# Causal attention between two feed-forward blocks: which of two score tiles comes first, and when VectorE reads it

## The chip, the core and the metric

The kernel runs on one core of a Trainium2 chip. The core has a matrix engine (TensorE, "PE" in the profile, with its weight loads as "PEld"), a vector engine (VectorE, "DVE"), a scalar engine (ScalarE, "ACT"), GpSimd ("POOL") and a sync engine (SyncE, "SP") whose queue issues the DMA transfers here. Matrix products go to PSUM, which the kernel uses as eight banks of 128 partitions x 512 fp32. VectorE and ScalarE read them from there. The metric is the device time of one execution in microseconds, as the median of several runs. Everything is fp32, but for a small operand of zeros.

## The reference

The program computes `x + ffn/2`, then `x + attention`, then `x + ffn/2` again, over 16 sequences of 512 tokens and 256 channels. The change touches the attention alone:

```python
def _L0_attn_ref(x, Wq, bq, Wkv, bkv, Wo, bo):     # x: layernormed, 16 x 512 x 256
    q = x @ Wq + bq                                  # H = 16 heads, DQK = DV = 64
    k, v = jnp.split(x @ Wkv + bkv, [H * DQK], axis=-1)
    q = _rope(q.reshape(b, s, H, DQK).transpose(0, 2, 1, 3))
    k = _rope(k.reshape(b, s, H, DQK).transpose(0, 2, 1, 3))
    v = v.reshape(b, s, H, DV).transpose(0, 2, 1, 3)
    scores = jnp.einsum('bhqd,bhkd->bhqk', q, k) * (1.0 / np.sqrt(DQK))
    scores = jnp.where(causal[None, None], scores, -jnp.inf)
    probs = jax.nn.softmax(scores, axis=-1)
    out = jnp.einsum('bhqk,bhkd->bhqd', probs, v)
    return out.transpose(0, 2, 1, 3).reshape(b, s, H * DV) @ Wo + bo
```

## The kernel before

**Units.** The work is cut into 64 units: a sequence and a group of four of its 16 heads (`units`, `HG = 4`). A unit's 512 queries are four tiles of 128 (0 to 3). Since the mask is causal, tile i needs only the first (i + 1) x 128 keys, so its score rows are 128, 256, 384 and 512 wide.

**The loop.** One loop (`for u in range(-2, nu)`, `L1221`) runs over the units as a pipeline, and each turn works on several units at once. In this part of the program the order of the instructions on every engine is the order in which the source writes them: nothing is rescheduled. In a usual turn TensorE does, in this order:

- `sums(u, 0)` and `sums(u, 1)` (`L1162`): probabilities times values for unit u, `p_av`, one bank for two heads; ScalarE moves each bank to `oT` by three activations (`L1183`);
- the scores of tiles 3 and 2 of unit u + 2, each in four banks, one a head (`scores`, `by_halves`, `L1063` and `L1070`);
- `leave(u, 0)` and `leave(u, 2)` (`L1185`): the output product `p_ay`, a bank each, which VectorE adds to `x` later in the turn (`L1196`);
- queries and keys of unit u + 3, four banks (`L988`); the values of unit u + 1, two banks (`L1010`); the scores of tiles 1 and 0 of unit u + 2, four banks (`L1048`).

That makes 22 banks a turn. They are handed out in turn from a ring of eight (`ps`, `L56`), so each product takes the bank of the one made eight before it, and waits until that one has been read. In the turn before the change, `leave(u, 0)` takes the bank of head 0 of tile 3, `leave(u, 2)` that of head 1, and heads 2 and 3 of tile 2 take the banks of the two `sums`.

**A score tile by halves.** For tiles 2 and 3, `by_halves` makes a head's 128 queries as two sides of 64, on the two column halves of the array, and the four heads lie on four groups of 32 rows. The later queries need 64 more keys than the earlier ones, so the sides are 320 and 384 wide for tile 2, and 448 and 512 for tile 3. Where the short side lacks 64 columns, a matmul of zeros (`blank`, `L1063`) fills them first. All four blanks of a tile come ahead of its other matmuls. For tile 3 the sides are swapped (`turned`), so that the side with the blank is the upper half there and the lower half in tile 2. The loop `for half in (1, 0)` gives the order in which the two sides are issued.

**Softmax.** `exps` (`L1074`) goes by head: VectorE scales and masks the scores out of the bank and takes the row's extreme (`L1086`), ScalarE does the exponential and its row sum (`L1090`). `scaled` (`L1093`) takes the reciprocals on VectorE and multiplies the rows on GpSimd (`L1098`).

**Turning.** The probabilities must be transposed for `sums`. VectorE turns blocks of 32 x 32 into `sq` (`L1113`): `turn_most` for a head's tiles 2 and 3, `turn_corner`, `turn_tile(1)` and `turn_tile(0)`. Then `move` (`L1132`) issues 16 DMA transfers on SP that put the blocks in place in `prT` (`L1140`). There is one buffer of `sq` for the unit being moved, so `turn_most(0)` of the next unit, at the end of the turn, waits for these transfers.

**VectorE's order around the change** (`old` is unit u + 1, `new` is unit u + 2): turns of `old` up to `turn_corner` and `turn_tile(1)`; the read of head 0 of `new`'s tile 3; `turn_tile(0)` and `move`; the reads of heads 1, 2 and 3 of tile 3; the four reads of tile 2, with the reciprocals of tile 3 halfway; the two additions of `p_ay`; the reciprocals of tile 2; the token statistics; the rotations of q and k (`L994`); `turn_most(0)`; the reads of tiles 1 and 0.

Of the kernel before, what the change touches and what calls it, by code (L numbers as in the profile page):

```python
# [34 lines left out]
HG = 4  # L35
# [12 lines left out]
def macaron_kernel(ctx: ExitStack, tc: tile.TileContext, a: dict, out: bass.AP):  # L48
# [836 lines left out]
    def attention(qp, wq, wk, wv, wo, cos, sin, row):  # L885
# [25 lines left out]
        nu = len(units)  # L911
# [19 lines left out]
        def enter(b):  # L931

            hs[b] = [qp.tile([P, 2, D], F32, tag=f"rope{2 + k}", name=f"h{b}_{k}") for k in range(2)]
            for t in range(NT):
                i = (b % PB) * NT + t
                nc.scalar.activation(hs[b][t // 2][:, t % 2, :], xs[b][:, t, :], AF.Identity,
                                     bias=shifts[b // PB][:, i:i + 1], scale=rstds[b // PB][:, i:i + 1])
# [5 lines left out]
        def width(b):  # L943
            hTs[b] = qp.tile([P, NC, S], F32, tag="hT", name=f"ahT{b}", bufs=2)
            for c in range(NC):
                pt = ps(f"p_ahT{b}_{c}")
                for t in range(NT):
                    nc.tensor.transpose(pt[:, t * P:(t + 1) * P], hs[b][t // 2][:, t % 2, c * P:(c + 1) * P], ident)
                nc.scalar.copy(hTs[b][:, c, :], pt)  # L949
# [52 lines left out]
        def values(u, t0):  # L1002
            b, hg = units[u]
            if t0 == 0:
                pool, tag, bufs = (ap, "v", 1) if u + 1 < nu else (qp, "hT", 2)
                vs[u] = pool.tile([P, NT, HG * DQ], F32, tag=tag, name=f"v{b}_{hg}", bufs=bufs)
            pv = ps(f"p_v{b}_{hg}_{t0}")
            for t in range(2):
                for k in range(NC):
                    nc.tensor.matmul(pv[:, t * 256:(t + 1) * 256], hTs[b][:, k, (t0 + t) * P:(t0 + t + 1) * P],  # L1010
                                     wv[:, k, hg * HG * DQ:(hg + 1) * HG * DQ],
                                     start=(k == 0), stop=(k == NC - 1))
            nc.scalar.copy(vs[u][:, t0:t0 + 2, :].rearrange("p t d -> p (t d)"), pv)  # L1013
# [8 lines left out]
        class Weights:  # L1022
# [33 lines left out]
            def by_halves(self, i, q, k, banks, at):  # L1056


                w, turned = (i + 1) * P, int(i == NT - 1)
                early = slice(turned * H, (turned + 1) * H)  # L1060
                for j in range(HG):
                    zero = blank[j * 32:(j + 1) * 32, :]
                    nc.tensor.matmul(banks[j][early, at + w - H:at + w], zero, zero, start=True, stop=True)  # L1063
                for n in range(2):
                    for j in range(HG):
                        rows = slice(j * 32, (j + 1) * 32)
                        for half in (1, 0):
                            late = half ^ turned
                            q0, wh = i * P + late * H, w - (1 - late) * H
                            nc.tensor.matmul(banks[j][half * H:(half + 1) * H, at:at + wh],  # L1070
                                             q[n][rows, q0:q0 + H], k[n][rows, :wh],
                                             start=(n == 0), stop=(n == 1))
# [131 lines left out]
        def queries_keys(u):  # L1204

            if u >= nu:
                return []
            q = qs[u] = Rotated(u, "q", wq, R_BQ)
            k = ks[u] = Rotated(u, "k", wk, R_BK)
            return [lambda: q.half(0), lambda: (q.half(1), q.add()), lambda: k.half(0), lambda: (k.half(1), k.add())]  # L1210
# [7 lines left out]
        with tc.tile_pool(name="awayh", bufs=2, space=bass.MemoryType.DRAM) as away, \  # L1218
                tc.manual_schedule(engines={mybir.EngineType.DVE, mybir.EngineType.Activation,
                                            mybir.EngineType.Pool, mybir.EngineType.SP}):  # L1220
            for u in range(-2, nu):  # L1221
                new = ws[u + 2] = Weights(u + 2) if u + 2 < nu else None
                qk = queries_keys(u + 3)
                old = ws.get(u + 1)

                fresh = units[u + 5][0] if NHG < u + 5 < nu and units[u + 5][1] == 0 else 1 if u + 3 == NHG else None

                stats = [divmod(at, NHG) for at in range(seen, min(u + 15, NB * NHG))]
                seen = max(seen, u + 15)
                left = [divmod(u - NHG - 1, NHG)] if u >= NHG + 1 else []  # L1230
                if u + 2 == nu:
                    old.scaled((1, 0))
                    values(u + 1, 0)
                    values(u + 1, 2)
                if u >= 0:
                    sums(u, 0)
                    sums(u, 1)
                if fresh:
                    enter(fresh)
                if u + 4 in trips:  # L1240
                    trips[u + 4].land((0, 1))
                if u + 3 in trips:
                    trips[u + 3].land((2, 3))
                if old and u + 2 == nu:
                    old.turn_at_once("sq", range(0, 10, 2))
                elif u == -1:
                    values(0, 0)
                    values(0, 2)
                    old.turn_at_once("prT", range(2, 10, 3))
                elif old:  # L1250
                    old.scaled((1, 0), slice(0, HG // 2))
                    old.turn_most(1)
                    old.turn_most(2)
                    old.scaled((1, 0), slice(HG // 2, HG))
                    old.turn_most(3)
                    old.turn_corner()
                    old.turn_tile(1)
                if new:
                    new.scores((3,))
                    new.scores((2,))  # L1260
                    new.exps((3,), slice(0, 1))
                if old and 0 <= u < nu - 2:
                    old.turn_tile(0)
                    old.move()
                if new:
                    new.exps((3,), slice(1, 2))
                gone = [leave(u, 0)] if u >= 0 else []
                if fresh == 1:
                    width(1)
                if u >= 0:  # L1270
                    gone.append(leave(u, 2))
                if new:
                    new.exps((3,), slice(2, HG))
                    new.exps((2,), halfway=lambda: new.scaled((3,)))
                if u == -2:
                    new.scaled((2,))
                    new.scores((1, 0))
                    new.exps((1, 0))
                    new.scaled((1, 0))
                if u + 6 in stds:  # L1280
                    scales((u + 6) // (PB * NHG), stds.pop(u + 6))
                if fresh and fresh > 1:
                    trips[u + 5] = Trip(fresh)

                if u == nu - NHG + 1:
                    for g in range(NB // PB - 1):
                        pair_rstd(g)
                if u == nu - 1:
                    for g in range(PB):
                        entered[g] = xs[g]  # L1290
                        for t in range(NT):
                            i = (g % PB) * NT + t
                            nc.vector.tensor_scalar(xs[g][:, t, :], xs[g][:, t, :], mvs[g // PB][:, i, 0:1],
                                                    rstds[g // PB][:, i:i + 1], ALU.subtract, ALU.mult)
                for one in gone:
                    one()
                if new and u > -2:
                    new.scaled((2,))
                for one in stats + left:
                    token_stats(*one)  # L1300
                for one in qk:
                    one()
                if fresh:
                    with_bias(fresh)
                if NHG < u + 7 < nu and (u + 7) % (PB * NHG) == 0:
                    stds[u + 7] = spread((u + 7) // (PB * NHG))
                if 0 <= u < nu - 2:
                    values(u + 1, 0)
                    values(u + 1, 2)
                if new and u > -2:  # L1310
                    new.scores((1, 0))
                    if u + 3 < nu:
                        new.turn_most(0)
                    new.exps((1, 0))
            token_stats(NB - 2, NT - 1)
# [55 lines left out]
```

## Time and profile before

| what | us |
|---|---|
| median of three runs | 2301.3 (2299.74 to 2306.26) |
| the profiled execution | 2299.63 |
| its span, first to last instruction | 2297.9 |
| one turn of the loop (1005.90 to 1029.16) | 23.26 |
| of it, `sums` to the scores of tile 3 (1007.42 to 1011.88) | 4.46 |
| the scores of tiles 3 and 2, to `p_ay` (1011.88 to 1015.19) | 3.31 |

The page gives, for each engine, the time in which it was busy over the whole program and its share of the span. The tables of windows give the same for stretches of time. A timeline line has the start and length of a merged group of instructions, and in brackets how long the engine had been idle before it and who released it. Matmuls are pipelined, and their ends are modelled: a following group can start a little before the end shown for the one ahead.

### The profile page before, as it was taken

The numbers are of one execution on the slowest core, as the hardware profiler recorded it, in microseconds if no ns is written. First come the engines' busy times: TensorE is split into PE (matmuls) and PEld (weight loads), VectorE is DVE, ScalarE is ACT, GpSimd is POOL, SyncE is SP. The second block draws the span as 40 slices with busy tenths as digits, with TensorE's granted clock in tenths as the row PEclk, the third lists the DMA queues.
The fourth block names the chain that finished last, engine by engine and source line by source line (L and its number), as shares of the span: only waits on it lengthen the run. The fifth ranks groups of instructions, "written<-read, shape, count | busy, mean of one in ns | idle before, by whom it ended". The sixth has DMA issues, their size and how long they took to land. (4 is left out here: it accounts for less than half of the span.)

```text
span 2297.9 us, 47763 instructions
## 1 busy us (share of the span) xinstructions
PE 2243.8 (98%) x16984; PEld 1463.8 (64%) x16984; DVE 1764.6 (77%) x4678; ACT 1158.2 (50%) x3296; POOL 1068.5 (47%) x1695
## 2 busy tenths in 40 slices
PE   7999999999999999999999999999999999998999
PEld 4764488666666666666666666666666666764588
DVE  5742298788989898989898998989888875432387
ACT  5753243555555555556465655555555565632233
POOL 2210053565566556565656565656656552210053
PEclk9999999999999999999999999999999999999999
DMA  6839851044545454454544454536454443839734
GB/s 213 260 108 406 347 141 56 9 131 120 135 123 152 107 153 127 125 139 112 146 130 129 129 143 110 159 97 163 119 134 129 124 116 113 238 141 406 306 117 141
DMA packets 221909, 359.19 MB, mean 156 GB/s; under 512 B 99876, under 2 KB 159848, under 8 KB 213480
## 3 DMA queue, kind: packets, MB, share of 16 engines
q1 hardware_dynamic: 220812, 355.34, 52.4%
q8 instruction: 135, 2.21, 0.4%
q10 hardware_dynamic: 860, 0.81, 0.1%
q14 instruction: 102, 0.84, 0.1%
HBM read 156.29 MB, written 37.22 MB: 84 GB/s over the span
## 5 line engine op out<-in xcount | busy, mean ns | idle before, releaser
L1098 POOL TENSOR_SCALAR pr<-pr,ars 128x512 f32<-128x512 f32 (+3 forms) x1024 | 524.1, 532 | 566.3 <-DVE ars L1095 565.3
L1090 ACT ACTIVATE pr<-pr,amn 128x512 f32<-128x512 f32 (+3 forms) x1024 | 561.9, 550 | 211.5 <-DVE amn L1086 207.1
L1113 DVE STREAM_TRANSPOSE sq<-pr 128x768 f32<-128x768 f32 x434 | 384.5, 918 | 78.6 <-DMA prT<-sq 54.8
L1013 ACT COPY v<-p_v 128x512 f32<-128x512 f32 x128 | 74.6, 585 | 449.4 <-PE p_v L1010 449.4
L1171 PE MATMUL p_av<-prT,v 128*64 128x512 f32 (+3 forms) x2048 | 289.8, 436 | 1.4 <-ACT pr L1090 1.4
L1086 DVE CUSTOM_DVE_ANT_1 pr<-p_as,causal 128x384 f32<-128x384 f32 (+1 forms) x512 | 237.8, 483 | 44.0 <-PE p_as L1048 43.6
L1190 PE MATMUL p_ay<-wo,aoT 128*128 128x256 f32 x1024 | 238.5, 386 | 12.0 <-DVE amn L1086 12.0
L1086 DVE CUSTOM_DVE_ANT_0 pr<-p_as,causal 128x512 f32<-128x512 f32 (+1 forms) x512 | 235.2, 478 | 2.7 <-PE p_as L1070 2.7
L1190 PEld LDWEIGHTS p_ay<-wo,aoT 128*128 128x128 f32 x1024 | 189.4, 190 | 70.3 <-DVE amn L1086 46.9
L1010 PE MATMUL p_v<-wv,ahT 128*128 128x256 f32 x1024 | 231.6, 379 | 0.7 <-DVE x L1196 0.7
L988 PE MATMUL p_q<-ahT,wq 128*128 128x512 f32 x512 | 230.7, 593 | 0.2 <-ACT ahT L949 0.2
L1171 PEld LDWEIGHTS p_av<-prT,v 128*64 128x64 f32 x2048 | 137.3, 137 | 146.6 <-issue 107.6
L988 PE MATMUL p_k<-ahT,wk 128*128 128x512 f32 x512 | 230.4, 592 | 0.0
L1010 PEld LDWEIGHTS p_v<-wv,ahT 128*128 128x128 f32 x1024 | 194.7, 190 | 53.5 <-issue 22.2
L1070 PE MATMUL p_as<-k,q 32*64 32x448 f32 (+3 forms) x4096 | 198.9, 517 | 0.0
L1090 ACT ACTIVATION_READ_ACCUMULATOR pr<-pr,amn 128x1 f32 x1024 | 192.0, 187 | 0.0
L988 PEld LDWEIGHTS p_k<-ahT,wk 128*128 128x128 f32 x512 | 97.4, 190 | 121.9 <-issue 106.6
L988 PEld LDWEIGHTS p_q<-ahT,wq 128*128 128x128 f32 x512 | 97.2, 190 | 95.5 <-issue 76.5
L1070 PEld LDWEIGHTS p_as<-k,q 32*64 32x64 f32 x4096 | 109.3, 131 | 29.0 <-issue 24.4
L1183 ACT ACTIVATE aoT<-p_av,bcol 128x64 f32<-128x64 f32 (+1 forms) x384 | 117.2, 392 | 7.7 <-PE p_av L1171 7.7
L811 PE MATMUL p_cy<-vw,catT 128*128 128x256 f32 x512 | 120.8, 380 | 0.0
L584 PE MATMUL p_ds<-hT,qk 128*128 128x512 f32 x256 | 118.7, 609 | 2.1 <-ACT hT L159 2.1
(181 smaller groups left out, 3501.7 us busy)
## 6 DMA issues: line engine op xcount, KB each, us to landing
prT<-sq SPq DMA_DIRECT2D x992, 160.0 KB
w<-in_e_W_dram SPq DMA_DIRECT2D x64, 1024.0 KB
w<-in_e_Wg_dram SPq DMA_DIRECT2D x32, 1024.0 KB
out_dram<-x SPq DMA_DIRECT2D x64, 256.0 KB
awaya<-sqa SPq DMA_DIRECT2D x25, 512.0 KB
atT<-awaya SPq DMA_DIRECT2D x100, 128.0 KB
xl<-in_attn_x_dram SPq DMA_DIRECT2D x16, 512.0 KB
xl<-out_dram SPq DMA_DIRECT2D x16, 512.0 KB
```

Source lines behind the costliest of these rows:

```text
L584: nc.tensor.matmul(psc, qk[:, k, c * P:(c + 1) * P], hT[:, k, :], start=(k == 0), stop=(k == NC - 1))
L811: nc.tensor.matmul(py[:, t * D:(t + 1) * D], atT[:, c, t * P:(t + 1) * P], vws[b][:, c, :], start=(c == 0), stop=(c == NC - 1))
L988: nc.tensor.matmul(pq, self.w[:, k, at:at + P], hTs[self.b][:, k, :], start=(k == 0), stop=(k == NC - 1))
L1010: nc.tensor.matmul(pv[:, t * 256:(t + 1) * 256], hTs[b][:, k, (t0 + t) * P:(t0 + t + 1) * P], wv[:, k, hg * HG * DQ:(hg + 1) * HG * DQ], s ...
L1070: nc.tensor.matmul(banks[j][half * H:(half + 1) * H, at:at + wh], q[n][rows, q0:q0 + H], k[n][rows, :wh], start=(n == 0), stop=(n == 1))
L1086: nc.vector.tensor_tensor_reduce(out=by_block(self.at(i, j)), in0=by_block(banks[j][:, at:at + w]), in1=mask(i), scale=-1.0 / math.sqrt(DQ ...
L1090: nc.scalar.activation(self.at(i, j), self.at(i, j), AF.Exp, bias=self.mn[:, i, j:j + 1], scale=-1.0, accum_out=self.rs[:, i, j:j + 1])
L1098: nc.gpsimd.tensor_scalar(self.at(i, j), self.at(i, j), self.rs[:, i, j:j + 1], 1.0, ALU.mult, ALU.mult)
L1113: nc.vector.transpose(view(self.sq, j * blocks * SQ + dst[0] * SQ, [(blocks * SQ, nh)] + [(s * SQ, n) for s, (_, n) in zip(dst[1:], of)] + ...
L1171: nc.tensor.matmul(po[j * DQ:(j + 1) * DQ, :].rearrange("d (a f) -> d a f", a=NSQ)[:, :, t * SQ:], vs[u][:, t, head * DQ:(head + 1) * DQ], ...
L1183: nc.scalar.activation(dst[:, to, tiles], src[:, of, tiles], AF.Identity, bias=bcol[:, r:r + 1])
L1190: nc.tensor.matmul(py[:, t * D:(t + 1) * D], oTs[u][:, pair, (t0 + t) * P:(t0 + t + 1) * P], wo[:, hg * (HG // 2) + pair, :], start=(pair ...
```

## The change

Tile 2's scores are made ahead of tile 3's, and its heads are read, exponentiated and scaled first. `turn_tile(1)` of the old unit moves behind the first head's read, so that VectorE reads head 0 of tile 2 right after `turn_corner`, and then turns tiles 1 and 0 together. The reciprocals of tile 2 are taken halfway through tile 3's reads, and those of tile 3 after the additions of `p_ay`. In `by_halves` the sides are issued lower half first. All counts of instructions stay as they are on every engine.

```diff
@@ by_halves
-                        for half in (1, 0):
+                        for half in range(2):
@@ the loop over u
                     old.turn_most(3)
                     old.turn_corner()
+                if new:
+                    new.scores((2,))
+                    new.scores((3,))
+                    new.exps((2,), slice(0, 1))
+                if old and 0 <= u < nu - 2:
                     old.turn_tile(1)
-                if new:
-                    new.scores((3,))
-                    new.scores((2,))
-                    new.exps((3,), slice(0, 1))
-                if old and 0 <= u < nu - 2:
                     old.turn_tile(0)
                     old.move()
                 if new:
-                    new.exps((3,), slice(1, 2))
+                    new.exps((2,), slice(1, 2))
...
-                    new.exps((3,), slice(2, HG))
-                    new.exps((2,), halfway=lambda: new.scaled((3,)))
+                    new.exps((2,), slice(2, HG))
+                    new.exps((3,), halfway=lambda: new.scaled((2,)))
                 if u == -2:
-                    new.scaled((2,))
+                    new.scaled((3,))
...
                 if new and u > -2:
-                    new.scaled((2,))
+                    new.scaled((3,))
```

## The prediction

> **What bounds the kernel now.** I read the page's engine totals first, then the waits over the attention stage (400 to 1900 us), then one turn of its loop in windows, and last that turn's timelines. The turn I use runs from one `L1048` group to the next, 1005.90 to 1029.16: 23.26 us, and 43 turns filled 1000 us, so it is the common case.
>
> ```profile
> PE 2243.8 (98%) x16984; PEld 1463.8 (64%) x16984; DVE 1764.6 (77%) x4678; ACT 1158.2 (50%) x3296; POOL 1068.5 (47%) x1695
> ```
> ```profile
> 1005.90:1029.16 23.26, 23.07 (x185) 14.42 (x185) 20.73 (x58) 11.96 (x40) 16.94 (x26) 1.00 0.61 153
> 1011.88:1015.19 3.31, 3.12 (x74) 1.87 (x73) 3.31 (x7) 1.50 (x6) 1.62 (x4) 1.00 0.00 0
> 1015.19:1029.16 13.97, 13.97 (x48) 9.05 (x49) 12.42 (x32) 6.02 (x17) 9.66 (x12) 1.00 0.78 198
> ```
> In the windows the columns are length, then busy time of PE, PEld, DVE, ACT, POOL. TensorE is idle for 0.19 us of a turn, all of it in the second window, which holds the scores of tiles 3 and 2. So the loop is bound by TensorE and by one wait on it. The waits name it (total us, times, longest):
>
> ```profile
> PEld p_ay L1190 <- DVE amn L1086: 46.9, 62, 0.9
> PE p_ay L1190 <- DVE amn L1086: 12.0, 62, 0.2
> PE p_as L1063 <- ACT aoT L1183: 2.5, 2, 1.8
> ```
> The output product `p_ay` takes the PSUM bank that held head 0 of tile 3's scores and waits, in 62 turns, until VectorE has read it. The third line is a wait that is nearly absent. It matters below.
>
> ```profile
> 1011.88 0.22 PE L1063 MATMUL p_as<-blank 32*64 32x64 bf16 x4
> 1013.66 0.21 PE L1063 MATMUL p_as<-blank 32*64 32x64 bf16 x3
> 1013.71 1.29 PE L1070 MATMUL p_as<-k,q 32*64 32x320 f32 x27
> 1015.19 3.72 PE L1190 MATMUL p_ay<-wo,aoT 128*128 128x256 f32 x16 [0.19 <-DVE amn L1086]
> ```
> ```profile
> 1011.82 2.73 DVE L1113 STREAM_TRANSPOSE sq<-pr 128x768 f32<-128x768 f32 x3
> 1014.47 0.65 DVE L1086 CUSTOM_DVE_ANT_0 pr<-p_as,causal 128x512 f32<-128x512 f32 x1
> 1015.05 0.71 DVE L1113 STREAM_TRANSPOSE sq<-pr 128x512 f32<-128x512 f32 x1
> ```
> Tile 3's scores occupy TensorE from 1011.88 to 1013.66, tile 2's to 1015.00. VectorE turns three pieces until 1014.55, the last being tile 1, then reads head 0 until 1015.12. `p_ay` follows at 1015.19.
>
> **The change, part by part.**
>
> *Read before turn (gain).* `turn_tile(1)`, the 128x1024 transpose, costs 1.245 us (53.5 us over 43) and leaves the path to `p_ay`. A 384-wide read (0.546 us) replaces a 512-wide one (0.669). VectorE is free for it at 1014.55 - 1.25 = 1013.31 and would finish by 1014.0. What `p_ay` would then wait for is its own engine. At three other changes of matmul shape the next group starts 0.07 us before the modelled end of the last: `p_v` 1005.97 to `L1048` 1005.90, `L1048` 1007.49 to `p_av` 1007.42, `p_av` 1011.95 to blanks 1011.88. So without the wait `p_ay` starts at 1014.93, a gain of 0.26 us a turn and 62 x 0.26 = 16.1 us in all, if nothing else ends later.
>
> *Tile 2 before tile 3 (loss).* The banks go round in turn. One turn takes 22 of them and there are eight, so the last two heads of whichever tile is scored second get the banks of the two `sums`, which ScalarE empties in `L1183`. The blank matmuls of that tile must wait for it.
>
> ```profile
> 1011.56 1.82 ACT L1183 ACTIVATE aoT<-p_av,bcol 128x384 f32<-128x384 f32 x6
> ```
> ```profile
> 1012.38 0.17 PEld L1070 LDWEIGHTS p_as<-k,q 32*64 32x64 f32 x4
> 1012.81 0.17 PEld L1070 LDWEIGHTS p_as<-k,q 32*64 32x64 f32 x4
> 1013.24 0.14 PEld L1063 LDWEIGHTS <-blank 32*64 32x64 bf16 x4 [0.26 <-issue]
> 1013.44 0.19 PEld L1070 LDWEIGHTS p_as<-k,q 32*64 32x64 f32 x5
> ```
> ScalarE's six evacuations end at 1013.38. The blanks' weights have been loaded from 1013.24 on, but the second tile's first weights only at 1013.44, 0.06 us after ScalarE: the sequence already stops there for that bank. It costs nothing today because tile 3, the wider one, keeps the array streaming until 1013.46 on one side (448-wide passes at 1012.34, 1012.71, 1013.09, so 0.375 each) and 1013.66 on the other (512-wide, 0.43 each). There is about 0.02 us to spare.
>
> After the change the tile in front is the narrow one. In proportion a 384-wide pass takes 0.32 us and a 320-wide one 0.27. Each side makes four passes per head (two halves of the head's width, two passes each). The 384 side runs out at 1011.90 + 0.05 + 4 x 0.32 = 1013.23, the 320 side at 1011.93 + 0.03 + 4 x 0.27 = 1013.04. ScalarE is no earlier. Its chain starts when VectorE reads `L1048`'s scores and runs without a gap (eight exponentials from 1008.03 to 1011.56, then 1.82 us), and the change touches neither. So the second tile starts at 1013.44, and now it is tile 3 with 512-wide passes:
>
> - first pass 1013.44, the next 0.48 later (the first 512-wide pass of today's tile 3 starts at 1011.90 and the second at 1012.38), then 0.43 and 0.43: the fourth starts at 1014.78;
> - the fourth head is 0.04 later: 1014.82. A 512-wide pass is modelled at 0.59 us, so the end is 1015.41, and `p_ay` starts 0.07 before it, at 1015.34.
>
> That is 0.15 us later than 1015.19. Gain and loss together: 62 x 0.15 = +9.3 us. The profiled execution took 2299.6 us (span 2297.9 and 1.7 around it), which gives 2308.9. The median of the runs shown is 1.7 higher, so the forecast for a median is 2310.6.
>
> Bounds of the terms that no row shows. The restart after the wait is at best free and at worst 0.10: `p_ay`'s first two passes take 0.70 us from 1015.19 and one is 0.38, so the second starts after 0.32, while the 16 passes in 3.72 us leave 0.22 for each later one. The start ahead of the modelled end was seen at other shapes alone: 0 to 0.12 us. With both at their best `p_ay` starts at 1015.24 and the sum is +3; with both at their worst at 1015.46, +17. I take 0.05 (same shape, first tile) and 0.07 (three changes of shape that agree).
>
> The rows at 1013.24 and 1013.44 show that weights for the other side of the array, and for heads whose banks had long been free, stood behind one waiting blank. [...] I go by the rows.
>
> *New order of sides.* `half` in (1, 0) becomes 0, then 1. In the built program the wide side still alternates: the first tile issues the side with the blank first, the second tile the other. Each side streams 320 + 512 or 384 + 448 columns, 832 as before. I cost it at nothing. If a side were left unpaired, one narrow pass, 0.27 us, would show each turn.
>
> *VectorE's queue.* The first read now waits for tile 2's head 0: last 384-wide pass from about 1012.92, 0.49 long, so 1013.41 against 1013.31 when VectorE is free. Wait and shorter read nearly cancel, so `turn_tile(0)` and the 16 transfers of `move()` on SP, first issued at 1015.82, shift by 0.0 to 0.1. Behind them `turn_most(0)` waits for those transfers, and after it VectorE still waits for `L1048` (0.86 us in this turn, 0.31 at 1054.03). That idle time hides the shift, and a turn that is 0.15 longer adds to it. Without it a shift of 0.1 would cost 6 us. The second `p_ay` needs head 1 of tile 2, read by about 1016.4, and starts near 1017.2.
>
> *GpSimd and ScalarE.* Four 384-wide and four 512-wide scalings, exponentials and reciprocals change places and keep their sums. GpSimd's eight scalings end at 1023.85 today and q's sums start at 24.31, after VectorE. Hidden, unless the second reciprocal comes over 0.46 later.
>
> **The rivals.**
>
> 1. *The removed wait is the whole story: faster.* The chance needs ScalarE's banks to be free in time or issue to pass the blank. Then `p_ay` starts at 1014.93: 62 x 0.26 = 16 us, 2285. For it: the table of waits hardly shows `L1063 <- ACT`. Against: the loads at 1013.44. It decides from the point where ScalarE's last evacuation ends before 1012.98, 0.4 us earlier than now. Chance 0.12.
> 2. *The two waits cancel: no change.* The stop is there, but the restart is free, or the weights that follow are ready behind the blank. [...] From my rows the low bound is +3, and up to +6 counts as no change: 2301 to 2308. Chance 0.22.
> 3. *VectorE becomes late for `turn_most(0)`.* The wait for tile 2 adds to the transfers' time. If the cover of 0.31 us failed by 0.1 in all turns, 6 more us: 2317. Against: a longer turn widens the cover. Chance 0.06.
>
> **How the numbers follow.** Forecast (the stop at the second tile takes the place of the wait, and outweighs it) 0.60. A measurement of this kernel tells about 0.3%, 7 us. Faster: rival 1, 0.12. Same: rival 2 and a little of the forecast's lower edge, 0.24. Slower: 0.64. The range reaches from no change, 2300, to both worst bounds, 2318; only rival 1 is left out.
>
> **What would show it.** In the profile after: the wait of `p_ay` on `DVE amn` is gone, and a wait of `L1063` or `p_as` on `ACT aoT` stands in some 62 turns. The turn is 23.41 us. The second tile's first weights still come 0.06 after ScalarE's sixth evacuation, about 1.56 after the first blank, and `p_ay` starts about 3.46 after it (3.31 now). I am wrong if the turn is below 23.26: then blanks do not hold what follows them, or ScalarE got earlier.

## The result, and the profile after

The changed kernel takes 2308.93 us in the median of seven runs, the kernel before 2299.74 in seven runs taken with them: a ratio of 1.0040 with a 95% interval of [1.0029, 1.0051]. It is slower by 9.2 us. The profiled execution has a span of 2304.3 us.

The table of windows for one turn (1007.67 to 1031.08), then its scores and the rest. The columns are length and busy time of PE, PEld, DVE, ACT and POOL:

```profile
1007.67:1031.08 23.41, 23.41 (x186) 14.14 (x185) 20.63 (x58) 11.96 (x40) 16.91 (x25) 1.00 0.59 149
1013.64:1017.10 3.46, 3.46 (x74) 1.60 (x72) 3.32 (x7) 2.22 (x8) 1.62 (x4) 1.00 0.00 0
1017.10:1031.08 13.98, 13.98 (x53) 9.04 (x49) 12.57 (x32) 5.31 (x15) 9.80 (x12) 1.00 0.77 198
```
The turn grew from 23.26 to 23.41 us. The whole 0.15 lies in the window of the scores, 3.31 before and 3.46 now; the others are the same within 0.01. And yet TensorE now counts as busy for all of the 23.41, where before it was idle for 0.19. This is the trap of this case: the time lost is not idle in the table.

The timelines of TensorE, of its weight loads and of ScalarE and VectorE show where it went:

```profile
1013.64 0.22 PE L1063 MATMUL p_as<-blank 32*64 32x64 bf16 x4
1013.66 1.54 PE L1070 MATMUL p_as<-k,q 32*64 32x384 f32 x32
1015.00 0.39 PE L1063 MATMUL p_as<-blank 32*64 32x64 bf16 x4
1015.20 1.97 PE L1070 MATMUL p_as<-k,q 32*64 32x512 f32 x32
1017.10 3.72 PE L1190 MATMUL p_ay<-wo,aoT 128*128 128x256 f32 x16
```
```profile
1014.68 0.14 PEld L1063 LDWEIGHTS <-blank 32*64 32x64 bf16 x4
1015.20 0.24 PEld L1070 LDWEIGHTS p_as<-k,q 32*64 32x64 f32 x16 [0.38 <-issue]
1017.10 0.30 PEld L1190 LDWEIGHTS p_ay<-wo,aoT 128*128 128x128 f32 x2 [0.81 <-DVE sq L1113]
```
```profile
1013.32 1.83 ACT L1183 ACTIVATE aoT<-p_av,bcol 128x384 f32<-128x384 f32 x6
```
```profile
1015.26 0.56 DVE L1086 CUSTOM_DVE_ANT_1 pr<-p_as,causal 128x384 f32<-128x384 f32 x1
1015.74 1.83 DVE L1113 STREAM_TRANSPOSE sq<-pr 128x1024 f32<-128x1024 f32 x2
```
Tile 2 runs from 1013.66. The blanks of tile 3 have their weights from 1014.68 on, and at 1015.00 the blanks that need not wait run. ScalarE's six evacuations end at 1015.15. At 1015.20 the last blank goes, and with it the first weights of tile 3. The weight loads had stood still for 0.38 us. That holds for the other side of the array too, though it had run dry by about 1014.80 (an estimate: its last 320-wide passes start from 1014.53, and the ones before them came 0.27 apart). In each of 61 turns of either kernel's trace the second tile's first weights come 0.05 us after ScalarE's last evacuation. From there to `p_ay` it takes 1.90 us. VectorE read head 0 by 1015.82, so `p_ay` has long stopped waiting for it.

The waits (400 to 1900 us) name none of this plainly:

```profile
PEld p_ay L1190 <- DVE sq L1113: 49.5, 61, 0.8
PEld p_as L1070 <- issue: 45.7, 186, 0.8
PE p_as L1063 <- ACT aoT L1183: 2.6, 2, 1.9
```
The wait on ScalarE is listed with two times only, as before the change. In the turn shown the modelled ends of the matmuls ahead reach to 1015.20 and cover it, and what remains is idle weight loading put down to "issue": 45.7 us where it was 24.4 (3 gaps a turn instead of 2). The first line names a transpose for which `p_ay` does not wait: in the turn shown the two end at 1017.57, and `p_ay` starts at 1017.10.

### The profile page after: what moved, and what is told of

It reads as the page before. It is cut to its first block, busy times and chain, and to the rows that moved or that the text cites. A ratio compares the mean times of both kernels' runs of the same rounds, so it can differ in the third digit from the quotient of the medians.

```text
span 2304.3 us, 47701 instructions
## 1 busy us (share of the span) xinstructions
PE 2259.1 (98%) x16984; PEld 1444.1 (63%) x16984; DVE 1762.3 (76%) x4678; ACT 1158.5 (50%) x3296; POOL 1069.0 (46%) x1695
## 5 line engine op out<-in xcount | busy, mean ns | idle before, releaser
L1098 POOL TENSOR_SCALAR pr<-pr,ars 128x384 f32<-128x384 f32 (+3 forms) x1024 | 525.1, 532 | 587.7 <-DVE ars L1095 582.4
L1090 ACT ACTIVATE pr<-pr,amn 128x384 f32<-128x384 f32 (+3 forms) x1024 | 561.7, 550 | 212.2 <-DVE amn L1086 212.2
L1070 PE MATMUL p_as<-k,q 32*64 32x384 f32 (+3 forms) x4096 | 223.8, 519 | 0.0
L1070 PEld LDWEIGHTS p_as<-k,q 32*64 32x64 f32 x4096 | 93.2, 131 | 56.9 <-issue 45.7
```

The lines of the kernel that those rows point to most:

```text
L1090: nc.scalar.activation(self.at(i, j), self.at(i, j), AF.Exp, bias=self.mn[:, i, j:j + 1], scale=-1.0, accum_out=self.rs[:, i, j:j + 1])
L1098: nc.gpsimd.tensor_scalar(self.at(i, j), self.at(i, j), self.rs[:, i, j:j + 1], 1.0, ALU.mult, ALU.mult)
```

## The experiments

Each is compared with the kernel before, run on the same chip with it. A turn is measured from one `p_av` group to the next around 1000 us.

**Each half of the change alone.** First the later turn of tile 1 without the new order of tiles (the diff is condensed, without its `if` lines):

```diff
 old.turn_corner()
-old.turn_tile(1)
 new.scores((3,)); new.scores((2,)); new.exps((3,), slice(0, 1))
+old.turn_tile(1)
 old.turn_tile(0)
```


> One part of the change alone: tile 3 stays first, and only turn_tile(1) goes behind the read of head 0. My theory (the change removes a wait worth 0.26 us a turn and pays 0.41 for having the narrow tile in front): the loss is gone and part of the gain is kept. VectorE is free at 1013.31 and has to wait for tile 3's head 0 until about 1013.85, reads it by 1014.5, so p_ay starts 0.26 earlier. But the read of head 1 ends about 1016.9, and the second p_ay wants its bank at 1016.8, and the 16 transfers start 0.5 later. So a turn of 23.0 to 23.2 instead of 23.26, total about 2287 to 2296. Rival (the later turn of tile 1 is what cost time in the change, by way of VectorE and the transfers, and the order of the tiles is harmless): slower than before, above 2300.

Measured: 2302.64 us, ratio 1.0016 [1.0008, 1.0025], a turn of 23.30. The total missed my range, and it falls where the rival put it. The trace settles it:

```profile
1015.68 0.69 DVE L1086 CUSTOM_DVE_ANT_0 pr<-p_as,causal 128x512 f32<-128x512 f32 x1 [0.52 <-PE p_as L1070]
1016.30 1.83 DVE L1113 STREAM_TRANSPOSE sq<-pr 128x1024 f32<-128x1024 f32 x2
1018.05 0.65 DVE L1086 CUSTOM_DVE_ANT_0 pr<-p_as,causal 128x512 f32<-128x512 f32 x1
```
```profile
1013.70 0.22 PE L1063 MATMUL p_as<-blank 32*64 32x64 bf16 x4
1016.75 4.02 PE L1190 MATMUL p_ay<-wo,aoT 128*128 128x256 f32 x16
```
`p_ay` starts 3.05 after the first blank, 0.26 earlier than before: the gain is there in full. Then its 16 passes take 4.02 us instead of 3.72. Both transposes now stand between the reads of heads 0 and 1, head 1 is read only by 1018.70, and the second `p_ay` needs that bank. So 0.26 is won and 0.30 lost. The mechanism was in my expectation; its size was not (0.1 late, and the restart left out): the ninth pass starts 0.41 us after the eighth, where 0.22 is usual, and the tenth comes another 0.10 late. So here VectorE does hold the loop, by its read of head 1, as the rival's reason has it in part; the transfers cost nothing that the turn shows. For the change itself that reason fails. There the narrow tile's head 1 is read by 1018.02, 0.92 us after `p_ay` starts, and the 16 passes run their 3.72 without a stop.

Then the new order of tiles without the early read, `old.turn_tile(1)` again ahead of `new.scores` in the changed kernel:

> The other part alone: tile 2 first, but tile 1 turned ahead of the first read as before. My theory: p_ay is held by its own engine until 3.46 us after the first blank, and VectorE would have read the bank by about 3.3 even after turning tile 1, so reading early is worth nothing with this order of tiles: a turn of 23.41 and 2309, the same as the whole change. Rival (the early read still brings something inside the change): slower than the changed kernel, a turn above 23.45.

Measured: 2309.17 us, 1.0042 [1.0030, 1.0055], a turn of 23.41. The same as the whole change. One line is worth learning from:

```profile
PEld p_ay L1190 <- DVE amn L1086: 50.7, 62, 1.2
```
The table blames VectorE's read in 62 turns, more than before the change (46.9). But in this run that read ends at 1018.38 and `p_ay` starts at 1018.72, when the scores end. The read was only the last release that the profile could see. It costs nothing here.

**Take away what the second tile waits for.** The three activations per `p_av` bank become one, in the changed kernel and, as a control, in the kernel before:

```diff
-for to, of, tiles in ((slice(0, 4), slice(0, 4), slice(0, NT - 1)), ...):
-    nc.scalar.activation(dst[:, to, tiles], src[:, of, tiles], AF.Identity, ...)
+nc.scalar.activation(dst, src, AF.Identity, bias=bcol[:, r:r + 1])
```


> The changed kernel with ScalarE's three activations per bank of p_av made into one over the whole bank. The two halves of the last query tile are then left in swapped order, so the output differs; counts on the other engines stay. The six activations take 1.82 us; two of 128x512 should take about 1.3, so ScalarE ends 0.5 earlier, before the narrow tile runs out. My theory (the blank's wait for ScalarE is the whole loss): the second tile starts on time, p_ay about 3.07 after the first blank, a turn of about 23.0, total about 2285. Rival (TensorE itself takes longer with the wide tile last, or the blanks on the other side hold it): the turn stays between 23.2 and 23.41, total 2299 to 2309.

> Control for the run before it: the kernel before with the same single activation per bank (the halves of the last query tile left swapped). My theory: before the change ScalarE is just in time and p_ay waits for VectorE, so an earlier ScalarE brings nothing: a turn of 23.26 and 2300, within 0.2%. Rival (a shorter ScalarE chain helps by itself, through later exponentials): the turn falls below 23.15 here too, under 2293.

Measured: the changed kernel falls to 2283.88 us, 0.9935 [0.9922, 0.9948], a turn of 23.00. The kernel before stays at 2298.39, 0.9993 [0.9984, 1.0002], 23.26. The timelines of the first:

```profile
1003.94 1.25 ACT L1181 ACTIVATE aoT<-p_av,bcol 128x512 f32<-128x512 f32 x2
```
```profile
1004.26 0.22 PE L1063 MATMUL p_as<-blank 32*64 32x64 bf16 x4
1007.31 3.72 PE L1188 MATMUL p_ay<-wo,aoT 128*128 128x256 f32 x16
```
And of the kernel before with the short evacuation:

```profile
1011.99 0.13 PEld L1070 LDWEIGHTS p_as<-k,q 32*64 32x64 f32 x1
```
```profile
1010.78 0.22 PE L1063 MATMUL p_as<-blank 32*64 32x64 bf16 x4
1014.09 3.72 PE L1188 MATMUL p_ay<-wo,aoT 128*128 128x256 f32 x16 [0.19 <-DVE amn L1086]
```
In the changed kernel ScalarE is now done at 1005.19, 0.93 after the first blank instead of 1.51, and `p_ay` starts 3.05 after it. So with tile 2 in front TensorE is not slower by itself. The whole 0.41 us a turn between 3.05 and 3.46 is the wait for ScalarE, and the control shows that a shorter ScalarE alone brought nothing here, where VectorE's read is last (0.19 us of idle time before `p_ay`). The control also bears out how the prediction read the kernel before: the first weights of its second tile now come 1.21 after the first blank instead of 1.56, so it was ScalarE that held them, and `p_ay` still starts at 3.31.

**The order of the sides.** In the changed kernel `for half in range(2)` goes back to `(1, 0)`:

> The changed kernel with the old order of sides, upper half first. My theory: at the second tile both sides have run dry and wait for the same evacuation, so it makes no difference which is issued first there: a turn of 23.41 to 23.43, 2309 to 2310. Rival (a side out of order costs 0.2 whatever stands before it): 23.6, 2321.

Measured: 2309.16 us, 1.0033 [1.0022, 1.0045], a turn of 23.42. No difference, as both sides stand still at the second tile anyway.

**A version that keeps the gain.** Tile 3 stays first. The short transpose goes ahead of the first read, the long one behind it, and GpSimd prepares the short one's input first:

```diff
 old.turn_corner()
-old.turn_tile(1)
+old.turn_tile(0)
 new.scores((3,)); new.scores((2,)); new.exps((3,), slice(0, 1))
-old.turn_tile(0)
+old.turn_tile(1)
 old.move()
 ...
-                    for i in tiles:            # in scaled()
+                    for i in sorted(tiles):
```


> A version meant to beat both: tile 3 stays first, tile 0 (0.69 us) is turned before the read of head 0 and tile 1 (1.25 us) after it, and in scaled() GpSimd takes a head's tile 0 before its tile 1, so that turn_tile(0) finds its input ready. My theory: VectorE turns tile 0 from 1013.3 to 1013.9, just when tile 3's head 0 is complete, reads it by 1014.5 and head 1 by 1016.4, and the transfers start no later than now. Both p_ay then start without a wait: 3.05 after the first blank, a turn of 23.0, total about 2283. Rival (after the wait is gone the loop is held by VectorE or the transfers, or by the second p_ay as in the run with tile 3 read first): a turn of 23.15 to 23.3, total 2293 to 2302.

Measured: 2285.21 us, 0.9932 [0.9919, 0.9944], a turn of 23.00. It beats both kernels, by 15 us the one before. VectorE's and TensorE's timelines:

```profile
1008.21 2.13 DVE L1113 STREAM_TRANSPOSE sq<-pr 128x768 f32<-128x768 f32 x3
1010.27 0.68 DVE L1086 CUSTOM_DVE_ANT_0 pr<-p_as,causal 128x512 f32<-128x512 f32 x1
1010.88 1.24 DVE L1113 STREAM_TRANSPOSE sq<-pr 128x1024 f32<-128x1024 f32 x1
1012.04 0.65 DVE L1086 CUSTOM_DVE_ANT_0 pr<-p_as,causal 128x512 f32<-128x512 f32 x1
```
```profile
1008.28 0.22 PE L1063 MATMUL p_as<-blank 32*64 32x64 bf16 x4
1011.33 3.72 PE L1190 MATMUL p_ay<-wo,aoT 128*128 128x256 f32 x16
```
Head 0 is read by 1010.95 and head 1 by 1012.69, one transpose between them. `p_ay` starts 3.05 after the first blank and runs its 3.72 without a stop. As far as these runs show, the loop is now bound by TensorE's own work: two ways of removing both waits, this and the short evacuation, end at the same 23.00. The margin at ScalarE stays as thin as before, since tile 3 is again in front: the second tile's first weights come 1.56 after the first blank (1009.84 against 1008.28), as in the kernel before, where they follow ScalarE by 0.05.

Without the new order in `scaled()`:

> The same without the new order in scaled(). GpSimd then finishes tile 0 of head 3 only at 1013.6, turn_tile(0) waits 0.35, and the reads of heads 0 and 1 end 0.35 later. My theory: the first p_ay starts 0.06 late and the second waits some 0.1 and restarts: a turn near 23.2, total about 2295. Rival (GpSimd's order is of no account): the same as the run above, 2283.

Measured: 2294.41 us, 0.9968 [0.9957, 0.9979]. The turn shown is 23.12, a little better than expected. Its waits (400 to 1900 us) show the cause, a wait of `turn_tile(0)` on GpSimd in 62 turns, and the timelines how it reaches TensorE:

```profile
DVE sq L1113 <- POOL pr L1098: 18.7, 62, 0.3
```
```profile
1015.34 0.71 DVE L1113 STREAM_TRANSPOSE sq<-pr 128x512 f32<-128x512 f32 x1 [0.33 <-POOL pr L1098]
1015.98 0.65 DVE L1086 CUSTOM_DVE_ANT_0 pr<-p_as,causal 128x512 f32<-128x512 f32 x1
```
```profile
1013.54 0.22 PE L1063 MATMUL p_as<-blank 32*64 32x64 bf16 x4
1016.70 3.74 PE L1190 MATMUL p_ay<-wo,aoT 128*128 128x256 f32 x16
```
Head 0 is read by 1016.63, and `p_ay` starts 3.16 after the first blank instead of 3.05.

Last, that version with the sides of the change, `range(2)`, so that the order of sides no longer mirrors the order of tiles:

> The version with tile 0 turned first, and the sides issued lower half first as in the change, but with tile 3 in front: the order of the sides is then not the mirror of the order of the tiles. My theory (matmuls are issued in order, and one whose side is busy holds those behind it): of the second tile the 320 side is issued first, its side is busy until 0.2 later than the other, so the scores end 0.15 to 0.2 later: a turn of 23.15 to 23.2, total about 2294. Rival (the sides work independently, and their order is free): no difference from the same version with the old order of sides.

Measured: 2304.09 us, 1.0015 [1.0007, 1.0024], a turn of 23.35: 0.35 us worse than with the old order, twice what I expected. The starts of the passes of the second tile, from the trace, correct my picture:

```
512-wide, last of tile 3:     1015.60 1015.62 1015.63 1015.64
384-wide, first of tile 2:    1015.84 1015.84 1015.85 1016.22
320-wide, first of tile 2:    1016.06 1016.07 1016.09 1016.10
384-wide, last of tile 2:     1016.83 1016.85 1016.87 1017.24
```
The 320-wide passes are issued ahead of the 384-wide of their head and start only from 1016.06, behind the last 512-wide passes of their side (from 1015.60; in the changed kernel such passes start 0.43 apart). Still, three heads' 384-wide passes go past them at 1015.84. Only the fourth is held, 0.37 us behind the third, and it ends as much behind (1017.24 against 1016.87). So in this run the passes that stood behind a busy side did not hold all that followed; my expectation had said they would.

## Why the prediction was right

**The total** was forecast at +9.3 us and measured at +9.2: 2310.6 against 2308.93, where the runs of before had come down by 1.6 meanwhile. That it agrees to 0.1 is partly luck, as the interval reaches from +6.7 to +11.7. The turn is the better witness: 0.15 us longer, as forecast.

**The gain, 0.26 us a turn.** Right, and shown apart: with both waits gone `p_ay` starts at 3.05 instead of 3.31 and the turn is 23.00 instead of 23.26. Times 62 it is 16 us; the version with tile 0 turned first measures 15.

**The loss.** Right in place and size. The forecast had the second tile's weights 1.56 us after the first blank and `p_ay` at 3.46; the profile has 1015.20 - 1013.64 = 1.56 and 17.10 - 13.64 = 3.46. The two terms taken from neighbours, the restart (0.05) and the start ahead of the modelled end (0.07), can be read in the trace after. The first head's 512-wide passes start at 1015.20, 1015.68, 1016.11 and 1016.54, so the first interval is 0.05 longer than the others, and `p_ay` starts at 1017.10, 0.07 before the modelled end of the scores at 1017.17. That the wait for ScalarE is the cause is shown by the pair with the short evacuation.

**The other side of the array.** The forecast went by the rows, and for the blank that waits for a semaphore the changed kernel bears them out: the 512 side's weights did not come before the last blank's wait had ended, at 1015.20. For passes whose side was merely busy the last experiment shows three of four heads going past them (at 1015.84) and the fourth 0.37 later, so there my expectation that such a pass holds those behind it was right in part only.

**The order of sides.** Costed at nothing: right for the change, with the reason a different one from mine. I argued that the mirror keeps the sides paired. It does: with the short evacuation the new order runs at 23.00. But in the changed kernel the wait at the second tile makes the order irrelevant in any case (23.41 and 23.42). In the version without a wait there the order was worth 0.35 us (23.35 against 23.00), not the 0.27 of a narrow pass that I named.

**VectorE, GpSimd, SP.** Right but for 0.09 us: the read of head 0 starts at 1015.26, 1.62 after the first blank (1.53 forecast), and the transfers' first issue comes 9.98 us after `L1048` instead of 9.92. Behind them nothing moved that the turn shows: its rest takes 13.98 us against 13.97.

**What would show it.** Half wrong. The turn, the loads and `p_ay` came as said, but I expected the wait of `L1063` on `ACT aoT` in 62 turns of the table, and it stands there in two. The stall hides behind the modelled ends of the matmuls ahead.

**The rivals.** That the removed wait is the whole story failed by 24 us, 2285 against 2309. That the two cancel failed too, if by little: the loss exceeds the gain by 0.15 us a turn. The weights were not ready behind the blank either: they came only at 1015.20, when its wait had ended, and the restart took 0.05. A VectorE late for `turn_most(0)` does not show: the rest of the turn kept its length.

## What to carry to other kernels

When a wait for a buffer is taken off the engine that bounds a loop, look which buffer the next instructions of that engine take and by how much it is free in time. Here the next one had 0.02 us to spare, and putting the narrower piece in front spent 0.41. The margin showed in the starts of the weight loads, 0.05 after the end of the releasing engine, and not in the table of waits, which with tile 2 first and tile 1 turned ahead named VectorE in 62 turns, though in the turn measured that read had ended 0.34 before `p_ay`. Moving the long operation behind a read did not help where the next read fell behind in its place (0.26 won, 0.30 lost): split what is moved so that no two reads have all of it between them.

## What the runs showed of the hardware

TensorE lost 0.41 us a turn in the changed kernel (`p_ay` 3.46 after the first blank, 3.05 with the short evacuation) and counted as busy throughout: 200.00 of 200 us from 1000 to 1200 us, against 198.47 before. A blank matmul that waited for a semaphore held the weight loads of the matmuls behind it, on both sides of the array: they stood still for 0.38 us in the changed kernel and began 0.05 us after ScalarE. In the last experiment 320-wide passes that stood behind a busy side until 1016.06 were overtaken by the 384-wide passes of three heads at 1015.84, and the fourth head's came 0.37 us later, in a run whose turn is 0.35 longer. Whether more than three can go by was not tried.
